# A graph attention network on one core: the order of the weight loads, the place of two weighed tiles, and a third transpose buffer

## The chip, the cores and the metric

The kernel runs on one core of a Trainium2 chip. The metric is the device time of one launch in microseconds. All durations below come from one profiled execution of the kernel before the change, unless a median of runs is named.

## What is computed

Two graph attention layers over 512 nodes with 768 features, then a residual and a layer norm. The first layer has eight heads, the second has one. Cut to what matters:

```python
def gat_layer(x, W, a_s, a_d, b, edge_index, concat):
    h = (x @ W).reshape(n, H, C)                       # 512 x 768 per head
    alpha_s = einsum('nhc,hc->nh', h, a_s)
    alpha_d = einsum('nhc,hc->nh', h, a_d)
    e = leaky_relu(alpha_s[src] + alpha_d[dst], 0.2)
    e = exp(e - segment_max(e, dst)[dst])
    alpha = e / (segment_sum(e, dst)[dst] + 1e-16)
    out = segment_sum(h[src] * alpha[:, :, None], dst)
    return out + b                                     # heads side by side

h   = elu(gat_layer(x, W1, a_src1, a_dst1, b1))        # W1: 768 x 6144
out = gat_layer(h, W2, a_src2, a_dst2, b2)             # W2: 6144 x 768
return layernorm(x + out)
```

## The kernel before

The edges are counted once into a dense 512 x 512 matrix `cnt` (from destination to source). With it the attention of one head is a dense softmax: `lift` adds the two logits into a tile `q[t]` of 128 destinations x 512 sources, `leak` and `rank` apply the leaky ReLU and the maximum on DVE and the exponential on ACT, and `weigh` multiplies by `cnt`, sums, and divides. There are four such tiles per head, t = 0 to 3. Each must then be transposed into `PT`. `turn_out` does the first half of that: ACT copies the tile into `nr` with its 16-bit halves apart (L548), and the SP queue issues a DMA transpose from `nr` into `zr` (L550). `turn_in` does the second half: ACT copies `zr` into `PT` (L553). Both `nr` and `zr` have two buffers, and the same names are used as scratch by `elu` and `mixed`.

The dense products are done by a scheme with seven half-size products in place of eight. A product is a sequence of fourteen "pairs": the seven products in the order P1, P2, P6, P7, P4, P5, P3, each for row blocks i = 0 and 1. A pair has a part on TensorE (six matmuls, L248) and an emptying part (DVE or ACT), called m and e here. P2 adds to the PSUM bank of P1, P4 to that of P7, P3 to that of P5, and each of these needs the bank's first result taken out before it starts. So P3 of block i cannot start until DVE has run L286, the emptying of P5, on the same block.

For each head there are three stages of TensorE work, and the loop over h runs them in this order for different heads:

- `mixed(h, ...)` (L625): attention times features of head h, then the ELU.
- `second(h, ...)` (L248, `gT` and `gS` operands): the result times the 768 x 768 block `W2[h]`, added into `h2`.
- `projection(h + 2, ...)` (L248, `xT` and `xS` operands): x times the block `W1[h + 2]`.

During `second(h)` the tiles `q[t]` of head h + 1 are made: the loop over n = 2 to 6 runs pairs 2n and 2n + 1, so that n = 5 holds P5 and n = 6 holds P3. Tiles 0 and 1 are weighed and turned out in n = 4 and 5. Tile 2 follows in n = 6, between the two emptyings of P3. Tile 3 follows in step n = 0 of the loop over `projection`. After it, in the same step, `load_w2(h + 1)` is issued.

A weight block is held in three tiles. `W[h][0]` and `W[h][1]` are its upper and lower 384 rows, loaded by three DMAs each. `t1` is a 384 x 384 block: first a copy of the upper left block by the SP queue (L109), then the upper right block added by an accumulating DMA on the POOL queue (L110), which must wait until the copy has landed. `rest` then adds the lower right block into the right half of `W[h][0]` with a second accumulating DMA (L115). The tiles of W1 are in the slots named `w2`, those of W2 in the slots named `w1`, and each slot has one buffer. So in the profile `w1t` is `t1` (and the sums t2 and t4) of a W2 block, and `w2t` the same of a W1 block. Two sums on DVE complete a block: L240 makes t2 from t1 and the lower right block, and L241 makes t4. For `W2[h + 1]` these two are put into the projection loop at steps n = 9 and 10, ahead of the emptyings of P5:

```python
                if n in (9, 10):
                    sums2.pop(0)()
```

The order of instructions on each engine is the order written in the program; nothing reorders them. The SP queue issues its DMAs in that order too, so a DMA that must wait for a buffer holds up those behind it.

Before the loop there is a head-0 phase. The first half of `projection(1)` is mixed with the counting; pairs 4 to 13 then run while head 0's four tiles are weighed and transposed, following the table `beside`. `load_w2(0)` is issued ahead of that phase. After pair 13 come `rsums` (L597 to L600), which make the sums of `PT` that `mixed(0)` needs.

In the last turn of the loop (h = 6) there is no projection. `load_w2(7, "w2")` loads into the W1 slots, and `a_src2` and `a_dst2` are loaded behind it. DVE then computes the logit vectors `V` from `W2[7]` (L702).

Of the kernel before, what the change touches and what calls it, by code (L numbers as in the profile page):

```python
# [8 lines left out]
F32 = mybir.dt.float32  # L9
# [3 lines left out]
U16 = mybir.dt.uint16  # L13
AF = mybir.ActivationFunctionType
ALU = mybir.AluOpType
# [21 lines left out]
def gat_pass(  # L37
# [16 lines left out]
    nc = tc.nc  # L54
    P = 128
    N, D = x.shape
# [4 lines left out]
    HALF = D // 2  # L61
    EC = E // P
    EH = EC // 2
    HK = DC // 2
    HN = N // 2
    L, R = slice(0, HALF), slice(HALF, D)
# [29 lines left out]
    W1, W2, A = {}, {}, {}  # L96

    def load_w(W, h, slot, m):


        W[h] = []
        for r in range(2):
            w = wpool.tile([P, HK, D], F32, name=f"{slot}{r}")
            for k in range(r * HK, (r + 1) * HK):
                nc.sync.dma_start(w[:, k - r * HK, :], m[k * P:(k + 1) * P, :])  # L105
            W[h].append(w)
        t1 = wpool.tile([P, HK, HALF], F32, name=f"{slot}t1")
        upper = m[:HK * P, :].rearrange("(k p) d -> p k d", p=P)
        nc.sync.dma_start(t1, upper[:, :, L])  # L109
        nc.gpsimd.dma_start(t1, upper[:, :, R], accum_op=ALU.add)  # L110
        W[h].append(t1)

        def rest():

            nc.gpsimd.dma_start(W[h][0][:, :, R], m[HK * P:, R].rearrange("(k p) d -> p k d", p=P),  # L115
                                accum_op=ALU.add)
        return rest
# [4 lines left out]
    def load_w2(h, slot="w1"):  # L122
        return load_w(W2, h, slot, w2[h * D:(h + 1) * D, :])
# [248 lines left out]
    def leak(q):  # L372
        nc.vector.scalar_tensor_tensor(q, q, NEG_SLOPE, q, op0=ALU.mult, op1=ALU.min)

    def rank(q, t):

        nmax = small.tile([P, 1], F32, name="nmax")
        nc.vector.tensor_tensor_reduce(out=q, in0=q, in1=absent[:, t, :], scale=1.0, scalar=-NO_EDGE,  # L378
                                       op0=ALU.add, op1=ALU.min, accum_out=nmax)
        nc.scalar.activation(q, q, AF.Exp, bias=nmax, scale=-1.0)  # L380
        return q
# [164 lines left out]
    def turn_out(q, t):  # L546
        apart = work.tile([P, N], F32, name="nr").bitcast(U16)
        nc.scalar.copy(apart.rearrange("p (h n) -> p h n", h=2), q.bitcast(U16).rearrange("p (n h) -> p h n", h=2))  # L548
        parted[t] = work.tile([P, N], F32, name="zr").bitcast(U16)
        nc.sync.dma_start(parted[t].rearrange("p (j d) -> p j d", d=P), apart, transpose=True)  # L550

    def turn_in(t):
        nc.scalar.copy(PT.rearrange("p s n -> p (s n)").bitcast(U16).rearrange("p (s n h) -> p s n h", s=NT, h=2)[  # L553
            :, :, t * P:(t + 1) * P, :], parted.pop(t).rearrange("p (h s d) -> p s d h", h=2, s=NT))

    def elu(h, c, z, cols, name, spare=None):

        j = h * DC + c
        n = z.shape[-1]
        neg = work.tile([P, n], F32, name=f"n{name}")  # L560
        pos = work.tile([P, n], F32, name=f"z{name}") if spare is None else spare
        nc.scalar.activation(neg, z, AF.Relu, bias=nb1T[:, j:j + 1], scale=-1.0)
        nc.scalar.activation(pos, z, AF.Relu, bias=b1T[:, j:j + 1])
        nc.scalar.activation(neg, neg, AF.Exp, scale=-1.0)
        return lambda: nc.vector.scalar_tensor_tensor(gT[:, c, cols], neg, -1.0, pos, op0=ALU.add, op1=ALU.add)
# [37 lines left out]
    def mixed(h, A_, B_, fill):  # L603

        tt = nc.vector.tensor_tensor
        behind = []

        def some(n):
            for f in fill[:n]:
                f()  # L610
            del fill[:n]

        for c in range(HK):
            u = work.tile([P, HN], F32, name="u")
            w = work.tile([P, HN], F32, name="w")
            zr = work.tile([P, N], F32, name="zr")
            bank = {}

            def part(p, over=None):
                if over is None:  # L620
                    bank[p] = mm.tile([P, 512], F32, name="mm")
                else:
                    bank[p] = bank[over]
                for k in range(2):
                    nc.tensor.matmul(bank[p][:, :HN], A_[p][:, k, c * P:(c + 1) * P], B_[p][:, k, :],  # L625
                                     start=over is None and k == 0, stop=k == 1, skip_group_check=True)
                return bank[p][:, :HN]

            nc.scalar.copy(u, part("P1"))  # L629
            if behind:  # L630

                behind = behind[0]()
            tt(u, u, part("P6"), op=ALU.add)
            tt(w, u, part("P7"), op=ALU.add)
            for f in behind[:1]:
                f()
            near_l = elu(h, c, part("P2", over="P1"), near, "l")
            some(1)
            tt(zr[:, far_], part("P5"), w, op=ALU.subtract)
            for f in behind[1:]:  # L640
                f()
            tt(zr[:, near], u, part("P4", over="P7"), op=ALU.add)
            near_l()
            tt(u, part("P3", over="P5"), u, op=ALU.subtract)
            some(-(-len(fill) // (2 * (HK - c) - 1)))

            def others(c=c, u=u, zr=zr):
                return [elu(h, HK + c, zr, slice(0, N), "r", spare=zr), elu(h, c, u, far_, "l", spare=u)]
            behind = [others]
        return behind[0]()  # L650

    load_a(1, a_src1[1], a_dst1[1])
    load_w2(0)()

    AA, lsums = left_sums(0)
    BB, rsums = right_sums()
# [2 lines left out]
    def give(t):  # L659
        weigh(q[t], t)  # L660
        turn_out(q[t], t)

    beside = {4: [lambda: give(0)], 7: [lambda: give(1)], 8: [lambda: leak(q[3]), lambda: rank(q[3], 3)],
              9: [lambda: turn_in(0), lambda: give(2)], 10: [lambda: turn_in(1), lambda: give(3)], 11: lsums[:1],
              12: [lambda: turn_in(2), *lsums[1:3]], 13: [lambda: turn_in(3), some_logits[0]]}
    for n in range(4, 14):
        pairs[n][0]()
        if n > 4:
            pairs[n - 1][1]()
        for f in beside.get(n, []):  # L670
            f()
    pairs[13][1]()
    for f in rsums:
        f()
    besides = [lsums[3], some_logits[1]]
    B2, pending = right(W2[0], "w1")
    for h in range(H - 1):
        if h + 2 < H:
            load_w1(h + 2)()
# [49 lines left out]
        for n in range(2, 7):  # L729
            (m0, e0), (m1, e1) = pairs[2 * n:2 * n + 2]  # L730
            m0()
            if not last:
                m1()
            if n < 6:
                leak(q[n - 2])
                rank(q[n - 2], n - 2)
            if n < 5:
                q.append(lift(h + 1, n - 1))
            if last:

                if n > 3:
                    turn(q[n - 4], n - 4)
                if n == 6:
                    weigh(q[3], 3)
                m1(lambda: turn(q[3], 3) if n == 6 else None)
            e0()
            if last and 2 < n < 6:
                weigh(q[n - 3], n - 3)
            if not last and n > 3:
                weigh(q[n - 4], n - 4)  # L750
                if n == 6:
                    turn_in(0)
                turn_out(q[n - 4], n - 4)
            e1()
        if h + 2 < H:
            B_, sums = right(W1[h + 2], "w2")
            pairs = projection(h + 2, XA, B_)
            for n in range(14):
                pairs[n][0]()
                if n == 0:  # L760
                    weigh(q[3], 3)
                    turn_in(1)
                    turn_out(q[3], 3)
                    load_w2(h + 1)()
                    B2, sums2 = right(W2[h + 1], "w1")
                if n in (1, 3):
                    sums[n // 2]()
                if n == 1:
                    AA, sums3 = left_sums(h + 1) if h + 3 < H else (None, [])
                pairs[n][1]()  # L770
                if n in (2, 4):
                    turn_in(1 + n // 2)
                if n == 5 and h + 3 < H:
                    BB, sums3 = right_sums()
                if 1 <= n < 9 and h + 3 < H:
                    sums3.pop(0)()
                if n in (9, 10):
                    sums2.pop(0)()
                if n in (11, 13):
                    logits(h + 2, HS[h + 2], 2 + (n - 11) // 2)  # L780
        else:
            last_sum()
            B2, sums2 = right(W2[H - 1], "w1")
# [151 lines left out]
```

## Time and profile before

| | us |
|---|---|
| median of 3 runs | 701.91 (701.33 to 703.17) |
| profiled execution | 701.47 |
| its span | 699.6 |
| TensorE busy | 663.7 |
| DVE busy | 511.7 |
| ACT busy | 248.3 |
| POOL busy | 41.8 |
| mean granted TensorE clock | 0.979 |

The span is the time from the first to the last recorded instruction; 1.87 us of the profiled execution lie around it. In the profile's rows, "L248" is a line of the kernel before, PE is TensorE's matmuls, PEld its weight loads, and a letter q after an engine means the engine's queue of DMA issues and waits. A DMA row in the chain of waits lasts from the issue to the landing. `mm` is a PSUM bank, `hs` the features of a head, `pS` the sums of `PT`.

### The profile page before, as it was taken

The page shows a single profiled execution, that of the slowest core. Times are in us where ns is not written, and L with a number is a line of the kernel's source. Part 1 is how long each engine was busy: PE and PEld are TensorE (multiplying, and loading weights), DVE is VectorE, ACT ScalarE, POOL GpSimd, SP SyncE. Part 2 cuts the span into 40 slices and gives each one's busy share as a digit, 9 for nine tenths or more (in the row PEclk, how much of TensorE's full clock was granted, in tenths as well). Part 3 has the DMA queues.
Part 4 walks back from the last instruction along what each step waited for, and adds up shares of the span by engine and source line. Part 5 has one row for each costly group of instructions (what it writes and reads, how often), then busy time and mean ns, then how long its engine had stood idle before and what let it go on. Part 6 is the DMA issues. An engine that isn't in the chain of part 4 may idle for free.

```text
span 699.6 us, 7102 instructions
## 1 busy us (share of the span) xinstructions
PE 663.7 (95%) x2419; PEld 406.5 (58%) x2419; DVE 511.7 (73%) x1102; ACT 248.3 (35%) x417; POOL 41.8 (6%) x52
## 2 busy tenths in 40 slices
PE   9999969997999989997999989997999989999995
PEld 4554557554865557554865567554865544554653
DVE  6899959965778577865778477775778179868685
ACT  2212536340545116340545116340545114234340
POOL 1200110001100101001100101001100101000000
PEclk9999989999999999999999999999999999999999
DMA  8705765076612855066612855076713866100021
GB/s 312 202 4 175 138 201 111 16 205 145 167 48 52 268 145 115 15 202 148 171 44 55 266 145 113 15 209 141 176 39 60 264 173 154 42 0 1 15 68 72
DMA packets 71355, 85.58 MB, mean 122 GB/s; under 512 B 36566, under 2 KB 55950, under 8 KB 71310
## 3 DMA queue, kind: packets, MB, share of 16 engines
q1 hardware_dynamic: 59022, 66.76, 30.9%
q0 software_dynamic: 12000, 17.70, 15.6%
q10 hardware_dynamic: 288, 0.59, 0.2%
q8 instruction: 21, 0.34, 0.2%
q14 instruction: 24, 0.20, 0.1%
HBM read 75.07 MB, written 1.57 MB: 110 GB/s over the span
## 4 chain that ended last, share of the span: by engine, by line
PE 76%; DMA 15%; DVE 4%; SPq 2%; issue 2%; ACT 1%; POOLq 0%; DVEq 0%; ACTq 0%
PE mm L248 42%; PE mm L625 16%; DMA w1t<-in_L_gnn_W_dram 13%; PE mm L571 5%; PE mm L352 5%; PE mm L887 3%; SPq L105 2%; PE tr L430 2%; DMA zr<-nr 2%; DVE w1t L240 1%; PE bc L154 1%; PE bc L430 1%; PE bc L363 0%; DVE scr L702 0%; DVE hs L286 0%
## 5 line engine op out<-in xcount | busy, mean ns | idle before, releaser
L248 PE MATMUL mm<-w,gT 128*128 128x384 f32 x288 | 97.7, 487 | 0.3 <-DVE u L306 0.3
L248 PE MATMUL mm<-w,xT 128*128 128x384 f32 x252 | 84.8, 489 | 0.0
L248 PEld LDWEIGHTS mm<-w,gT 128*128 128x128 f32 x288 | 53.4, 190 | 36.9 <-DVE u L306 2.6
L248 PEld LDWEIGHTS mm<-w,xT 128*128 128x128 f32 x252 | 47.2, 190 | 35.1 <-ACT hs L281 3.0
L248 PE MATMUL mm<-w1t,gS 128*128 128x384 f32 x180 | 60.7, 486 | 0.0
L248 PE MATMUL mm<-w,xS 128*128 128x384 f32 x84 | 39.0, 631 | 21.0 <-DVE hs L286 21.0
L629 ACT COPY u<-mm 128x256 f32<-128x256 f32 x18 | 6.7, 372 | 145.2 <-PE mm L625 145.2
L380 ACT ACTIVATE q<-q,nmax 128x512 f32<-128x512 f32 x36 | 25.8, 722 | 90.3 <-DVE nmax L378 90.3
L248 PE MATMUL mm<-w2t,xS 128*128 128x384 f32 x168 | 56.6, 487 | 0.0
L306 DVE TENSOR_TENSOR h<-h,mm 128x384 f32<-128x384 f32 x72 | 39.7, 551 | 20.5 <-PE mm L248 19.3
L625 PE MATMUL mm<-PT,hs 128*128 128x256 f32 x216 | 54.0, 387 | 0.0
L248 PEld LDWEIGHTS mm<-w1t,gS 128*128 128x128 f32 x180 | 34.1, 190 | 23.6
L625 PEld LDWEIGHTS mm<-PT,hs 128*128 128x128 f32 x216 | 42.1, 195 | 7.5 <-issue 0.4
L248 PEld LDWEIGHTS mm<-w2t,xS 128*128 128x128 f32 x168 | 31.8, 190 | 22.2 <-issue 0.2
L625 PE MATMUL mm<-pS,gS 128*128 128x256 f32 x144 | 38.0, 387 | 5.5 <-DVE pS L598 5.5
L248 PEld LDWEIGHTS mm<-w,xS 128*128 128x128 f32 x84 | 20.1, 245 | 39.8 <-DVE hs L286 24.7
L548 ACT COPY nr<-q 128x1024 uint16<-128x1024 uint16 x32 | 33.4, 1043 | 25.6 <-DVE q L534 25.6
L571 PE MATMUL mm<-PT,hs 128*128 128x512 f32 x96 | 41.6, 593 | 0.0
L553 ACT COPY PT<-zr 128x1024 uint16<-128x1024 uint16 x32 | 37.1, 1158 | 8.1 <-DMA zr<-nr 8.1
L418 DVE TENSOR_SCALAR os<-nodes,idx 128x512 bf16<-128x512 f16 x132 | 35.5, 340 | 3.6 <-PE tr L430 3.6
L625 PEld LDWEIGHTS mm<-pS,gS 128*128 128x128 f32 x144 | 27.8, 194 | 9.7 <-DVE pS L598 5.9
L352 PE MATMUL mm<-w,xT 128*128 128x384 f32 x96 | 33.2, 493 | 0.0
(158 smaller groups left out, 1048.1 us busy)
## 6 DMA issues: line engine op xcount, KB each, us to landing
w<-in_L_gnn_W_dram SPq DMA_DIRECT2D x90, 384.0 KB, 5.6
w<-in_L_gnn_W_dram POOLq DMA_DIRECT2D x15, 576.0 KB, 10.2
w2t<-in_L_gnn_W_dram SPq DMA_DIRECT2D x8, 576.0 KB, 6.1
w2t<-in_L_gnn_W_dram POOLq DMA_DIRECT2D x8, 576.0 KB, 6.3
w1t<-in_L_gnn_W_dram SPq DMA_DIRECT2D x7, 576.0 KB, 8.8
w1t<-in_L_gnn_W_dram POOLq DMA_DIRECT2D x7, 576.0 KB, 7.9
a_s<-in_L_gnn_a_src_dram SPq DMA_DIRECT2D x8, 384.0 KB, 6.8
a_d<-in_L_gnn_a_dst_dram SPq DMA_DIRECT2D x8, 384.0 KB, 6.3
```

What stands on the lines that cost most here:

```text
L105: nc.sync.dma_start(w[:, k - r * HK, :], m[k * P:(k + 1) * P, :])
L248: nc.tensor.matmul(ps[:, :HALF], A_[p][:, k, i * P:(i + 1) * P], B_[p][:, k, :], start=start and k == 0, stop=k == HK - 1, skip_group_chec ...
L306: nc.vector.tensor_tensor(a, a, ps, op=ALU.subtract if p == "P7" else ALU.add)
L352: nc.tensor.matmul(ps, xT[:, r * HK + k, t * P:(t + 1) * P], W1[h][r][:, k, cols], start=r == 0 and k == 0, stop=r == 1 and k == HK - 1)
L380: nc.scalar.activation(q, q, AF.Exp, bias=nmax, scale=-1.0)
L418: nc.vector.tensor_scalar(hot[c], nodes, idx[:, 1, c:c + 1], None, op0=ALU.is_equal)
L430: nc.tensor.matmul(cps[t][r:r + B, :N], od[:, c, k * B:(k + 1) * B], hot[c], start=todo[b] == hits[b], stop=todo[b] == 1, tile_position=(0 ...
L548: nc.scalar.copy(apart.rearrange("p (h n) -> p h n", h=2), q.bitcast(U16).rearrange("p (n h) -> p h n", h=2))
L553: nc.scalar.copy(PT.rearrange("p s n -> p (s n)").bitcast(U16).rearrange("p (s n h) -> p s n h", s=NT, h=2)[:, :, t * P:(t + 1) * P, :], p ...
L571: nc.tensor.matmul(ps[:, :N], HS[h][:, s, c * P:(c + 1) * P], PT[:, s, :], start=(s == 0), stop=(s == NT - 1))
L625: nc.tensor.matmul(bank[p][:, :HN], A_[p][:, k, c * P:(c + 1) * P], B_[p][:, k, :], start=over is None and k == 0, stop=k == 1, skip_group ...
L887: nc.tensor.matmul(ps[:, :cols.stop - cols.start], PT[:, s, t * P:(t + 1) * P], h2[:, s, cols], start=(s == 2), stop=(s == 1))
```

## The change

Four things are moved; every computation and every transfer stays.

1. In `load_w` the copy and the accumulation of `t1` come first, ahead of the six DMAs of `W[h][0]` and `W[h][1]`. This holds for W1 and W2 blocks alike.
2. In the loop, tile 2 is weighed and turned out ahead of the emptying of P3's block 0, and tile 3 between the two emptyings of P3, both in n = 6. `load_w2(h + 1)` follows there. The step n = 0 of the projection keeps only `turn_in(1)`.
3. In the head-0 phase `load_w2(0)` moves behind the issue of head 0's fourth transpose (n = 10). The tiles 2 and 3 are given one step earlier relative to the emptyings, and the `turn_in`s are placed anew.
4. `zr` gets a third buffer (in `turn_out`, and in the two other places that use the name, `elu` and `mixed`).

```diff
     def load_w(W, h, slot, m):
+        t1 = wpool.tile([P, HK, HALF], F32, name=f"{slot}t1")
+        upper = m[:HK * P, :].rearrange("(k p) d -> p k d", p=P)
+        nc.sync.dma_start(t1, upper[:, :, L])
+        nc.gpsimd.dma_start(t1, upper[:, :, R], accum_op=ALU.add)
         W[h] = []
         for r in range(2):
             w = wpool.tile([P, HK, D], F32, name=f"{slot}{r}")
             for k in range(r * HK, (r + 1) * HK):
                 nc.sync.dma_start(w[:, k - r * HK, :], m[k * P:(k + 1) * P, :])
             W[h].append(w)
-        t1 = wpool.tile([P, HK, HALF], F32, name=f"{slot}t1")
-        upper = m[:HK * P, :].rearrange("(k p) d -> p k d", p=P)
-        nc.sync.dma_start(t1, upper[:, :, L])
-        nc.gpsimd.dma_start(t1, upper[:, :, R], accum_op=ALU.add)
         W[h].append(t1)
...
-        parted[t] = work.tile([P, N], F32, name="zr").bitcast(U16)
+        parted[t] = work.tile([P, N], F32, name="zr", bufs=3).bitcast(U16)
...
     load_a(1, a_src1[1], a_dst1[1])
-    load_w2(0)()
...
-    beside = {4: [lambda: give(0)], 7: [lambda: give(1)], 8: [lambda: leak(q[3]), lambda: rank(q[3], 3)],
-              9: [lambda: turn_in(0), lambda: give(2)], 10: [lambda: turn_in(1), lambda: give(3)], 11: lsums[:1],
-              12: [lambda: turn_in(2), *lsums[1:3]], 13: [lambda: turn_in(3), some_logits[0]]}
+    done = {n: (lambda n=n: pairs[n][1]()) for n in range(4, 13)}
+    beside = {4: [lambda: give(0)], 5: [done[4]], 6: [done[5]], 7: [done[6], lambda: give(1)],
+              8: [done[7], lambda: leak(q[3]), lambda: rank(q[3], 3), lambda: turn_in(0)], 9: [lambda: give(2), done[8]],
+              10: [lambda: give(3), lambda: turn_in(1), done[9]], 11: [done[10], lsums[0]],
+              12: [done[11], lambda: turn_in(2), *lsums[1:3]], 13: [done[12], some_logits[0], lambda: turn_in(3)]}
     for n in range(4, 14):
         pairs[n][0]()
-        if n > 4:
-            pairs[n - 1][1]()
-        for f in beside.get(n, []):
+        for f in beside[n]:
             f()
+        if n == 10:
+            load_w2(0)()
+            B2, pending = right(W2[0], "w1")
...
+            if not last and n == 6:
+                turn_in(0)
+                weigh(q[2], 2)
+                turn_out(q[2], 2)
             e0()
             if last and 2 < n < 6:
                 weigh(q[n - 3], n - 3)
-            if not last and n > 3:
+            if not last and 3 < n < 6:
                 weigh(q[n - 4], n - 4)
-                if n == 6:
-                    turn_in(0)
                 turn_out(q[n - 4], n - 4)
+            if not last and n == 6:
+                weigh(q[3], 3)
+                turn_out(q[3], 3)
+                load_w2(h + 1)()
             e1()
...
                 if n == 0:
-                    weigh(q[3], 3)
                     turn_in(1)
-                    turn_out(q[3], 3)
-                    load_w2(h + 1)()
                     B2, sums2 = right(W2[h + 1], "w1")
```

More of the change, by code (lines that the diff above doesn't have):

```diff
@@ L560, in elu @@
         neg = work.tile([P, n], F32, name=f"n{name}")
-        pos = work.tile([P, n], F32, name=f"z{name}") if spare is None else spare
+        pos = work.tile([P, n], F32, name=f"z{name}", bufs=3 if name == "r" else 2) if spare is None else spare
         nc.scalar.activation(neg, z, AF.Relu, bias=nb1T[:, j:j + 1], scale=-1.0)
@@ L615, in mixed @@
             w = work.tile([P, HN], F32, name="w")
-            zr = work.tile([P, N], F32, name="zr")
+            zr = work.tile([P, N], F32, name="zr", bufs=3)
             bank = {}
@@ L675, in gat_pass @@
     besides = [lsums[3], some_logits[1]]
-    B2, pending = right(W2[0], "w1")
     for h in range(H - 1):
```

## The prediction

> **What bounds the kernel now.** I read the page first, then the waits of PE, then the chain of waits, then the timelines of SP, DVE and PE around one stall.
>
> ```profile
> PE 663.7 (95%) x2419; PEld 406.5 (58%) x2419; DVE 511.7 (73%) x1102; ACT 248.3 (35%) x417; POOL 41.8 (6%) x52
> ...
> PE mm L248 <- DVE hs L286: 21.0, 6, 4.0
> PE mm L625 <- DVE pS L598: 5.5, 1, 5.5
> ```
>
> TensorE is busy 95% of the span, and its idle time is nearly all in two places: six waits for L286 (once per turn of the loop with a projection) and one for `pS` in the head-0 phase. Only what shortens these can be worth much. The chain of waits in turn h = 1:
>
> ```profile
> 226.88 0.52 SPq L105
> ...
> 229.89 8.96 DMA w1t<-in_L_gnn_W_dram
> 238.92 0.48 issue
> 239.41 7.52 DMA w1t<-in_L_gnn_W_dram
> 246.96 1.36 DVE w1t L240
> 248.32 0.48 DVE hs L286
> 248.84 5.83 PE mm L248 x12
> 254.67 18.38 PE mm L625 x84
> ```
>
> SP issues six W DMAs, then the copy of `t1`; it lands after 8.96, POOL adds to it for 7.52, then DVE can run L240. L240 stands in DVE's order ahead of L286, which P3 needs. So P3 waits for a transfer that it does not use. Its own block then takes 5.83 instead of the 4.03 of the other blocks of twelve:
>
> ```profile
> 241.54 4.03 PE L248 MATMUL mm<-w2t,xS 128*128 128x384 f32 x12
> 248.84 5.83 PE L248 MATMUL mm<-w,xS 128*128 128x384 f32 x12 [3.27 <-DVE hs L286]
> ...
> 248.00:252.00 4.00, 3.16 (x7) 1.88 (x8) 3.96 (x7) 0.00 (x0) 0.00 (x0) 0.76 0.19 32
> ```
>
> The last row is a stretch of the windows view: the granted clock falls to 0.76 behind the stall. The head-0 phase in the chain:
>
> ```profile
> 75.81 9.39 DMA zr<-nr
> ...
> 89.37 3.05 DMA zr<-nr
> 92.45 1.17 ACT PT L553
> 93.64 0.70 DVE pS L597
> 94.36 0.70 DVE pS L598
> 95.11 20.38 PE mm L625 x80
> ```
>
> The first transpose lands after 9.39, the others' best is 3.05: it was issued while `load_w2(0)`'s two accumulations ran.
>
> **Part 1 and 2: the loop.** Worth at most: blocks of twelve start 3.87 apart when nothing waits (237.67, 241.54), so from the start of P5 to the start of `mixed` 7.74 are needed. The PE timeline shows 13.67, 12.97, 13.39, 12.74, 13.43 and 13.05 in the six turns; lost 5.93 + 5.23 + 5.65 + 5.00 + 5.69 + 5.31 = 32.8. That is idle time plus cold matmuls.
>
> How much earlier `t1` comes, in turn h = 1:
> - DVE. One `weigh` takes 1.51 (220.78 to 222.29). Tile 2's now starts where L306 of P5 ends, 218.97, and ends 220.5; P3's first emptying 221.0; tile 3's `weigh` 222.5 (before 224.3); the second emptying 223.0 (before 222.8). Projection's P1 needs neither of these two banks, so nothing waits for the 0.2.
> - ACT. `turn_in(0)` ends 220.65, tile 2's copy 221.7. Tile 3's copy needs the `nr` of tile 1, whose transpose goes out at 219.6 and takes 3.05: it runs 222.7 to 223.7. `turn_in(1)` now stands behind it and ends 224.9, then L281 ends 225.3; P2 needs that at 225.84. No wait.
> - SP. The last transpose goes out at 223.7 and occupies SP for 1.23. The third `zr` buffer is what lets tile 2's go out without waiting for `turn_in(0)`. `t1` is issued at 224.95 instead of 229.89. Its buffer is free: P5 of `second(1)` ended at 218.3. `W[h][1]`, used by P3 until 222.1, is free too. So SP is not blocked.
> - Copy of `t1`: between 4.0 (the single x tile on ACT's queue, smaller) and 8.96 (behind six others). It now has only a transpose in front; I take 5.0: landed 230.0, POOL's issue 0.5, accumulation from 230.5.
> - Accumulation: the row is 7.52, beside three W DMAs (longest 8.85, the shortest for `w2t` 5.7). Now up to six W DMAs share the queues. The Trainium skill, DMA: Bandwidth & Descriptors, section on queues, rings and completion order, says that each DMA engine takes turns between queues packet by packet, which speaks against this change: SP's burst, which stood before the accumulation, is now beside it. By the rule: 80 to 84 us moved 165 GB/s with the engines full of accumulations, so 0.59 MB is 3.6 of engine time; shared half and half 7.2, with about 2.7 for start and receipt (6.3 typical for `w2t`, less 3.6) 9.9: landed 240.4. By the row: 238.0. I take the rule's.
> - The six W DMAs (L240 reads `W[h][1]`): the same 2.95 MB start 1.9 earlier; the last landed by 238.85, now 236.9 plus 3.6 for the accumulation in between: 240.5.
>
> L240's place in DVE's order comes at 242.3, behind L285. P3 would start at 245.41, so L240 must start by 245.41 - 1.36 - 0.48 - 0.04 = 243.5. Data at 240.5 leave 3.0 of margin. Even 8.96 and 8.85 together give 224.95 + 8.96 + 0.48 + 8.85 = 243.3. So all of the stall goes: -32.8. L241 then lies between the two L286, which P3's second block needs only at 247.3. The next limit is PE's own stream.
>
> Also moved: `load_w1(h + 2)` now begins with `t1`, freed by P5 (245.4), so its six DMAs go out then instead of from 237.86 and 256. They are needed some 50 us later; behind them on SP are only `a_s` and `a_d`, and on POOL its two accumulations. Cost 0. The same reorder at the start (`load_w1(1)`) is needed at 63.2 and was in at 27.3 + 10.2 (POOL's last addition, median to landing) = 37.5: 0.
>
> **Part 3: head 0.** `mixed(0)` took 26.79 (88.54 to 115.33) against 18.38 later: 8.4 lost. Without accumulations beside it the first transpose lands in 3.05 (bounds: 1.23 or again 4.05 of issue, its own row). Copies follow at ACT's pace, the fourth transpose out at 84.0 to 85.4, `turn_in(3)` ends 88.3 to 89.7. DVE reaches `rsums` at 89.2, after L287 of pair 13, so L598 ends 90.4 to 91.0, while PE finishes P1 of `mixed` at 89.4: idle 1.1 to 1.7. The skill, TensorE: Matmul & The Clock Gate, Part 1, puts the cold clock behind an idle window of about 3.4; the trace shows it already behind 3.04 (turn h = 3). At 1.1 neither makes it cold; if it did, the 2.4 of before (5.04 for twelve matmuls worth 2.6) would stay. I take -7.0 (ends -4.5 and -7.3).
>
> `load_w2(0)` moves from 60.6 to about 85, with `load_w1(2)` right behind: 5.9 MB at 366 GB/s (window 232 to 236) is 16.1, four accumulations at 3.6 14.4; all is in by 118. `W2[0]` comes first in both queues, by about 103; P1 needs it at 110, L240 at 116. Cost 0; uncovered, each us late costs one.
>
> **The last turn.** `load_w2(7)` now starts with `t1`, which waits for P5 of the last projection. Before, `W[7][0]` was issued at P7's end (552.01), 17 us ahead of `W[7][1]`.
>
> ```profile
> 570.72 0.48 SPq L685 DMA_DIRECT2D w2t<-in_L_gnn_a_src_dram  x1
> ...
> 578.67 0.96 DVE L702 SCALAR_TENSOR_TENSOR scr<-w,w2t 128x768 bf16<-128x768 f32 x1 [0.37 <-DMA w2t<-in_L_gnn_a_dst_dram]
> ...
> 596.05 2.20 PE L248 MATMUL mm<-w,gT 128*128 128x384 f32 x6 [0.32 <-DVE u L306]
> ```
>
> DVE waits for `a_src2` and is then full until PE waits for it, so a later `a_src2` is paid in full. With E the end of P3: before, 568.7 + 9.9. Now `t1`, `W[7][0]`, `W[7][1]` and `a_src2` (3.3 MB, 9.1 at 366 GB/s) and 3.6 to 3.9 of accumulation run from E - 1.8: E + 11.2, with the receipt E + 12.2. Cost +2.3 (ends 0, if DMA has slack there, and +4).
>
> **Sum.** Against the profiled execution: 701.47 - 32.8 - 7.0 + 2.3 = 664.0. The median is 0.44 above it: 664.4. I predict 664.4.
>
> **The rivals.**
> - *Part of the wait stays.* The accumulation or `W[h][1]` lands 1 to 3 after the deadline, so L240 is still last. For: six W DMAs beside it have no row. Against: the 3.0 of margin. A stall of 2 per turn leaves 12, to 676; with the cold block 23, to 687. Chance 0.17.
> - *The accumulation is starved: slower.* Place: L240 in each of six turns. Decides: what head 0 and the last turn net is 7.0 - 2.3 = 4.7, 0.8 per turn; so if the data come over 0.8 later than before, past 247.8, all is lost. From 230.5 that is an accumulation of 17.3, twice the longest row. At 19 it is 1.7 x 6 = 10 minus 4.7: 707. For: POOL's is one ring against a queue of six loads. Against: in 240 to 244 it got its share beside three. Chance 0.05.
> - *The reorder moves nothing in the loop:* `W[h][1]` was the late one all along and lands when it did, with only head 0 gained: 701.9 - 4.7 = 697. Against: the waits name `w1t`, landed 8 us later. Chance 0.04.
>
> **Chances.** The forecast 0.74. About 0.3% (2 us) can be told from no change in this kernel. Faster 0.93, same 0.02 (starved just so), slower 0.05. The forecast's own ends: 701.9 - 32.8 - 7.3 = 661.8, and -32.8 - 4.5 + 4 = 668.6. PE's weight loads also waited 3.0 in all for L281, which comes 0.5 earlier in each turn: up to -3 more. The range takes in that end and the first half of the first rival: 659 to 679.
>
> **What would show it.** Right: no wait of PE for L286 over 0.5, block P3 at 4.03, `t1` issued by SP before the six W DMAs and 5 us earlier against P5, turns of 73.0 instead of 78.4, `mixed(0)` under 20, and L702 waiting about 2.5. Wrong: L240 waiting for `w1t` or `w` past the end of P5; PE waiting for W2's first block in `second(0)`; a granted clock under 0.95 in the middle of the loop.

## The result and the profile after

| | us |
|---|---|
| before, median of 4 runs beside it | 701.62 (701.21 to 703.17) |
| after, median of 4 runs | 661.37 (660.9 to 662.61) |
| ratio after / before | 0.9425, 95% interval 0.9405 to 0.9445 |
| profiled execution of after | 662.61 |
| its span | 660.8 (699.6 before) |
| mean granted TensorE clock | 0.996 (0.979 before) |

The page of after, first the engines, then the shares of the chain of work that ended last:

```profile
PE 649.1 (98%) x2419; PEld 401.1 (61%) x2419; DVE 511.7 (77%) x1102; ACT 248.6 (38%) x417; POOL 42.8 (6%) x52
...
PE 93%; DMA 3%; DVE 2%; issue 1%; SPq 0%; ACT 0%; DVEq 0%
```

TensorE runs the same 2419 matmuls in 14.6 us less busy time, nearly all of it because the blocks behind the old stalls are no longer cold: six times 1.8, and 2.3 in `mixed(0)`. The waits of PE in after (in total, times, longest):

```profile
PE mm L248 <- DVE u L306: 1.4, 2, 0.8
...
PE mm L625 <- DVE pS L598: 1.1, 1, 1.1
```

The row for L286 (21.0 us before) is gone, and the one for `pS` fell from 5.5 to 1.1. One turn of the loop in the chain of waits of after:

```profile
186.56 50.31 PE mm L248 x156
236.87 18.38 PE mm L625 x84
255.25 3.87 PE mm L248 x12
```

156 matmuls of `second` and `projection` follow one another without a gap, where before a transfer, a POOL addition, L240 and L286 stood in the middle. The same turn in the timelines, SP first, then PE, then DVE:

```profile
203.32 9.32 SPq L550 DMA_TRANSPOSE zr<-nr  x4
212.74 0.52 SPq L103 DMA_DIRECT2D w1t<-in_L_gnn_W_dram  x1
213.35 3.20 SPq L109 DMA_DIRECT2D w<-in_L_gnn_W_dram  x6
...
228.97 4.03 PE L248 MATMUL mm<-w2t,xS 128*128 128x384 f32 x12
232.84 4.03 PE L248 MATMUL mm<-w,xS 128*128 128x384 f32 x12
...
229.64 1.35 DVE L240 TENSOR_TENSOR w1t<-w1t,w 128x1152 f32<-128x1152 f32 x1
231.10 0.56 DVE L286 TENSOR_TENSOR hs<-mm,hs 128x384 f32<-128x384 f32 x1
```

`t1` is issued in front of the six loads, 16.23 ahead of P5's start (212.74 to 228.97; before 229.89 to 241.54, which is 11.65). A square bracket behind a row would name what the engine waited for; L240 carries none, so its data is there. Block P3 is at 4.03, and the first matmul of `mixed` starts at 236.71 in the PE timeline: 7.74 behind P5's start, the distance when nothing waits. (The chain, in which ends are followed, has 236.87 for it.)

How the 38.8 of span divide, each from the same two points of the PE timelines: the loop -32.8 (the six distances P5 to `mixed` are all 7.74); `mixed(0)` -6.8 (26.79 to 20.02); the first two blocks of `projection` -0.9 in all (8.05 to 7.90 in each of six turns, the weight loads' wait for L281); the last turn +1.3 (start of `mixed` to P6 of `second(7)`: 29.36 to 30.70); the start of the program +0.4.

### The profile page after: what moved, and what is told of

Read it like the earlier page. It is cut to its first block, busy times and chain, and to the rows that moved or that the text cites. A ratio compares the mean times of both kernels' runs of the same rounds, so it can differ in the third digit from the quotient of the medians.

```text
span 660.8 us, 7107 instructions
## 1 busy us (share of the span) xinstructions
PE 649.1 (98%) x2419; PEld 401.1 (61%) x2419; DVE 511.7 (77%) x1102; ACT 248.6 (38%) x417; POOL 42.8 (6%) x52
## 4 chain that ended last, share of the span: by engine, by line
PE 93%; DMA 3%; DVE 2%; issue 1%; SPq 0%; ACT 0%; DVEq 0%
PE mm L248 61%; PE mm L625 17%; PE mm L352 5%; PE mm L571 3%; PE mm L891 3%; PE tr L430 2%; DMA w2t<-in_L_gnn_a_dst_dram 2%; DMA hs<-in_x_dram 1%; DVE scr L703 1%; PE bc L430 1%; PE bc L363 0%; DVE gT L565 0%; PE mm L327 0%; PE tr L819 0%; PE tr L540 0%
## 5 line engine op out<-in xcount | busy, mean ns | idle before, releaser
L248 PE MATMUL mm<-w,gT 128*128 128x384 f32 x288 | 97.8, 488 | 1.4 <-DVE u L306 1.4
L248 PE MATMUL mm<-w,xT 128*128 128x384 f32 x252 | 83.9, 487 | 0.0
L248 PEld LDWEIGHTS mm<-w,gT 128*128 128x128 f32 x288 | 53.4, 190 | 38.2 <-DVE u L306 3.9
L248 PEld LDWEIGHTS mm<-w,xT 128*128 128x128 f32 x252 | 47.7, 190 | 33.7 <-issue 0.4
L248 PE MATMUL mm<-w1t,gS 128*128 128x384 f32 x180 | 60.7, 486 | 0.0
L248 PE MATMUL mm<-w2t,xS 128*128 128x384 f32 x168 | 56.6, 487 | 0.0
L625 PE MATMUL mm<-PT,hs 128*128 128x256 f32 x216 | 52.5, 379 | 0.0
L306 DVE TENSOR_TENSOR h<-h,mm 128x384 f32<-128x384 f32 x72 | 39.7, 551 | 13.9 <-PE mm L248 12.7
L248 PEld LDWEIGHTS mm<-w1t,gS 128*128 128x128 f32 x180 | 34.1, 190 | 23.6
L248 PEld LDWEIGHTS mm<-w2t,xS 128*128 128x128 f32 x168 | 31.8, 190 | 22.2 <-issue 0.2
L625 PEld LDWEIGHTS mm<-PT,hs 128*128 128x128 f32 x216 | 41.0, 190 | 6.9
L553 ACT COPY PT<-zr 128x1024 uint16<-128x1024 uint16 x32 | 37.1, 1159 | 2.0 <-DMA zr<-nr 2.0
L248 PE MATMUL mm<-w,gS 128*128 128x384 f32 x96 | 32.6, 486 | 0.0
L248 PE MATMUL mm<-w1t,gT 128*128 128x384 f32 x96 | 32.5, 487 | 0.0
L571 PEld LDWEIGHTS mm<-PT,hs 128*128 128x128 f32 x96 | 18.2, 190 | 22.9 <-issue 21.5
```

Source lines behind the costliest of these rows:

```text
L248: nc.tensor.matmul(ps[:, :HALF], A_[p][:, k, i * P:(i + 1) * P], B_[p][:, k, :], start=start and k == 0, stop=k == HK - 1, skip_group_chec ...
L306: nc.vector.tensor_tensor(a, a, ps, op=ALU.subtract if p == "P7" else ALU.add)
L571: nc.tensor.matmul(ps[:, :N], HS[h][:, s, c * P:(c + 1) * P], PT[:, s, :], start=(s == 0), stop=(s == NT - 1))
```

## The experiments

All are timed against the kernel before, run beside them on the same chip. In the first group one part of the change is made alone, in the kernel before.

**Part 1 alone: `t1` first in `load_w`.**

```diff
     def load_w(W, h, slot, m):
+        t1 = wpool.tile(...)
+        nc.sync.dma_start(t1, upper[:, :, L])
+        nc.gpsimd.dma_start(t1, upper[:, :, R], accum_op=ALU.add)
         W[h] = []
...
-        t1 = wpool.tile(...)
-        nc.sync.dma_start(t1, upper[:, :, L])
-        nc.gpsimd.dma_start(t1, upper[:, :, R], accum_op=ALU.add)
         W[h].append(t1)
```

> The kernel before with part 1 alone: t1 is copied and added first in every weight load; tiles, head-0 phase and zr buffers as before. Theory (L240 waits for t1, and the order of the load is enough): in turn h = 1 t1 is issued at 226.9 where the six W DMAs began, lands in 4.5, the accumulation takes about 9, so the data are there at 240.5 to 241.5, ahead of the 243.5 at which L240 must start. All 32.8 of the loop go, the last turn costs 1.3, head 0 keeps its loss or part of it: 664 to 670. Rival (the tiles' earlier place is what brings t1 forward): at most a third of the 32.8 goes: over 690.

Measured: 662.59 (662.25 to 662.81), ratio 0.9434 (0.9386 to 0.9483): as far as the intervals can tell, the whole change (0.9425). In turn h = 1, from its SP, POOL and DVE timelines:

```profile
214.41 0.52 SPq L103 DMA_DIRECT2D w1t<-in_L_gnn_W_dram  x1
...
219.35 1.28 POOL L104 DMA_DIRECT2D w1t<-in_L_gnn_W_dram  x1 [49.67 <-DMA w1t<-in_L_gnn_W_dram]
...
229.73 1.35 DVE L240 TENSOR_TENSOR w1t<-w1t,w 128x1152 f32<-128x1152 f32 x1
```

The reorder gains twice. `t1` is issued 14.65 ahead of P5's start (229.06) instead of 11.65, and its copy no longer lands behind six loads: 4.94 from issue to POOL's start, against 9.5 before (229.89 to 239.41). Together the accumulation can begin 7.6 sooner. Part 1 reorders the W1 blocks too: the next block's loads now go out at 233.60, where before three of them were issued 1.55 ahead of the accumulation, and part 2 below shows that such loads delay it. How much of the gain comes from that, no run separates.

It also mends head 0, which I had put down to part 3. `t1` of `W2[0]` is now first there as well, so the two accumulations start at 67.26 and 70.53 instead of at 73.44 and 74.23; POOL's queue has moved 0.83 MB of their 1.18 MB by 76, when the first transpose goes out (76.03), and the rest by 78. In the kernel before they run from 75 to 83. The DMA view of before for 76 to 82 (q0 is POOL's queue, q1 SP's; the columns are packets, MB and the time of the packets as a share of the 16 engines) shows what the first transpose, issued at 75.81, had to wait for:

```profile
q0 software_dynamic: 670, 1.00, 102.2%
q1 hardware_dynamic: 234, 0.06, 7.8%
```

The four transposes of `zr` in this phase, by the tile view of the kernel before:

```profile
DMA to landing us min/median/max: 3.0/5.3/9.4
```

and by that of part 1 alone:

```profile
DMA to landing us min/median/max: 3.1/3.4/3.6
```

The 9.4 is gone, L598 starts at 90.15 (before 94.36), and PE's wait for `pS` is 1.1, the same as in after.

**Part 2 alone, with the third buffer: tiles 2 and 3 weighed around P3, `t1` last.**

```diff
+            if not last and n == 6:
+                turn_in(0)
+                weigh(q[2], 2)
+                turn_out(q[2], 2)
             e0()
...
+            if not last and n == 6:
+                weigh(q[3], 3)
+                turn_out(q[3], 3)
+                load_w2(h + 1)()
             e1()
```

> The kernel before with part 2 alone: tiles 2 and 3 weighed around P3, load_w2(h + 1) behind them, third zr buffer; t1 is loaded last and the head-0 phase is as before. Theory: t1 is issued about 2 earlier than before, its data are there at about 245 to 246, 1.4 to 2.7 past the deadline, so L286 stays late but by less; 678 to 687 if a wait that short leaves TensorE's clock up, 690 to 697 if P3's block still takes 5.83. Rival (either part alone is enough): 669 or less.

Measured: 699.19 (694.67 to 702.69), ratio 0.9954 (0.9926 to 0.9982). Neither expectation holds. The profiled execution is the slowest of the ten (702.69), and in it the wait for L286 is not smaller at all:

```profile
PE mm L248 <- DVE hs L286: 21.6, 6, 4.1
```

Turn h = 1 in its chain of waits:

```profile
228.81 9.16 DMA w1t<-in_L_gnn_W_dram
...
238.53 9.69 DMA w1t<-in_L_gnn_W_dram
248.24 1.36 DVE w1t L240
```

P5 starts at 241.94 here, so `t1` is issued 13.13 ahead of it: 1.5 earlier than before, as planned. But the accumulation takes 9.69 where it took 7.52, and over all seven blocks the medians to landing are 8.7 and 9.4, against 8.8 and 7.9. What was won at the issue was given back in the accumulation. What differs beside it is the next block's first three loads (`load_w1`, issued when PE frees their buffer): before they were issued 1.55 ahead of the accumulation (237.86 and 239.41), here 0.27 ahead (238.26 and 238.53). The DMA view of this kernel for 238 to 243 shows the cause:

```profile
q1 hardware_dynamic: 340, 0.95, 67.1%
q0 software_dynamic: 1, 0.00, 0.2%
```

While these loads ran on SP's queue, the accumulation issued at 238.53 moved one packet; it ran from 243 on, when they were nearly over. In before the loads were over about a microsecond earlier, and POOL's queue began then, at 242 to 243. Where the 2.5 of the medians lies, this execution does not show, apart from 0.9 (the first two blocks of `projection` take 7.90 here too).

**Part 3 alone, with the third buffer: `load_w2(0)` behind the transposes and the new table `beside`.**

```diff
     load_a(1, a_src1[1], a_dst1[1])
-    load_w2(0)()
...
+        if n == 10:
+            load_w2(0)()
```

> The kernel before with part 3 alone: the head-0 phase and the place of load_w2(0) as in the changed kernel, with the third zr buffer; the loop and the order inside a load as before. Theory: the first transpose lands in about 3 instead of 9.4, mixed(0) takes 20.0 instead of 26.8, the loop's waits stay: 694.8. Rival (W2(0), now 25 later and with t1 last, is late for second(0)): 697 or more, with a wait of PE for L306 or for w in second(0).

Measured: 695.94 (694.08 to 697.56), ratio 0.9917 (0.9885 to 0.995). The `pS` wait is 1.1, the waits for L286 stay (22.5 in all). Standing alone, part 3 brings 5.8 of the 7.0 worked out for it; beside part 1 there is nothing left for it to win, since each gives the same 1.1.

**The sums later, nothing else.** L240 and L241 are moved behind both emptyings of P5 in DVE's order; no transfer moves.

```diff
-                if n in (9, 10):
+                if n in (12, 13):
                     sums2.pop(0)()
```

> The kernel before with one edit: the two sums of W2[h + 1] stand at steps 12 and 13 of the projection loop instead of 9 and 10; no transfer is moved. Theory (P3 waited only because L240 stood ahead of L286 in DVE's order): PE's wait for L286 is gone and P3's block takes 4.03; DVE then has 2.7 of sums to do where mixed begins, so a new wait in mixed of at most 2.7 in each turn: 680 to 688, or less if mixed has slack. Rival (the transfer itself bounds the turn): 699 to 702.

Measured: 674.2 (673.0 to 674.54), ratio 0.9598 (0.9547 to 0.9648). PE's waits in this kernel:

```profile
PE mm L625 <- DVE pS L598: 5.0, 1, 5.0
PE mm L625 <- DVE w L634: 2.7, 5, 0.5
```

Turn h = 1 in its PE timeline:

```profile
236.53 4.03 PE L248 MATMUL mm<-w2t,xS 128*128 128x384 f32 x12
240.40 4.03 PE L248 MATMUL mm<-w,xS 128*128 128x384 f32 x12
244.27 1.03 PE L625 MATMUL mm<-PT,hs 128*128 128x256 f32 x4
```

The waits for L286 are gone and P5 to `mixed` is 7.74, although `t1` is as late as ever. So the stall was not TensorE waiting for data: it was L286 standing behind an instruction that waited for data. The price is that the two sums now stand in front of L633 and L634, which `mixed` needs: PE waits for L634 in five turns, and `mixed` takes 19.54 (244.27 to 263.81) instead of 18.38. Head 0's wait stays, as nothing was done about it.

The second group undoes or adds one thing in the kernel after. On the chip of the first three of them after itself gave 661.46 (660.89 to 662.34) in a second run, ratio 0.9426 (0.9399 to 0.9452).

> The changed kernel once more, as the yardstick of the three runs beside it: 661.4.

Its last turn is 29.48 from `mixed` to P6 of `second(7)`, against 30.70 in the first profile of the same kernel and 29.36 before. So this stretch differs by 1.2 from one execution to another.

**`t1` last in `load_w2(7)` alone.**

```diff
     def load_w2(h, slot="w1"):
-        return load_w(W2, h, slot, w2[h * D:(h + 1) * D, :])
+        return load_w(W2, h, slot, w2[h * D:(h + 1) * D, :], late=h == H - 1)
```

(`late` puts the two DMAs of `t1` behind the six loads.)

> The changed kernel, but load_w2(7) in the last turn copies and adds t1 last, as before the change. Theory (t1 first holds up a_src2 in the last turn, and PE pays for it): L703 waits 0.4 instead of 2.1 and 1.0 to 1.4 is gained: 660.2. Rival (that delay is covered): no change, 661.4.

Measured: 661.49 (661.36 to 661.8), ratio 0.9424 (0.9398 to 0.9449); the last turn is 29.37. No difference in time that can be told.

**`a_src2` and `a_dst2` ahead of `load_w2(7)`.**

```diff
-            last_sum = load_w2(H - 1, "w2")
             A[H] = []
             for j, a in ((2, a_src2[0]), (4, a_dst2[0])):
...
+            last_sum = load_w2(H - 1, "w2")
```

> The changed kernel, with a_src2 and a_dst2 issued ahead of load_w2(7) instead of behind it. Theory: they land before L703 needs them, DVE does not wait there, and PE's two waits for L306 in the last turn (0.54 and 0.85) go: 1.4 to 2.0 gained, 659.6. Rival (W2[7]'s own rows come as late): no more than with the old order of t1, 660.2 or above.

Measured: 661.41 (661.26 to 661.97), ratio 0.9425 (0.9399 to 0.9451); the last turn is 29.36. No difference that can be told.

**The same, and L597 and L598 ahead of pair 13's emptying in head 0.**

```diff
+    for f in rsums[:2]:
+        f()
     pairs[13][1]()
-    for f in rsums:
+    for f in rsums[2:]:
         f()
```

> As the run before this one, and the first two sums of PT (L597, L598) stand ahead of the emptying of pair 13 in the head-0 phase. Theory: PE's wait of 1.1 for L598 shrinks to about 0.2, and everything else stays: 658.7. Rival (the bank that pair 13 holds longer is then missed by mixed): 659.6 or more.

Measured: 660.83 (660.65 to 661.18), ratio 0.9414 (0.9388 to 0.944). The `pS` wait fell from 1.1 to 0.3. It is the lowest median of all, 0.6 below after, about what one wait of 0.8 is worth. The ratios' intervals overlap, but they carry the scatter of the kernel before: all five runs lie below all five of the kernel without this last move (661.26 to 661.97).

**Two `zr` buffers instead of three**, in all three places that use the name; the cut shows one.

```diff
-        parted[t] = work.tile([P, N], F32, name="zr", bufs=3).bitcast(U16)
+        parted[t] = work.tile([P, N], F32, name="zr").bitcast(U16)
```

> The changed kernel with two zr buffers again. ACT's order has turn_in(0) ahead of tile 2's copy, but turn_in(1) behind tile 3's copy, so tile 3's transpose must wait for turn_in(1): about 1.1 later in each turn, and all loads with it. Theory: the margin in front of L240 covers it, head 0 loses 0.2 to 1.1: 661.4 to 662.5. Rival (the third buffer is needed): 665 or more.

Measured: 661.62 (660.96 to 662.8), ratio 0.9413 (0.9384 to 0.9443). The third buffer is not needed. In turn h = 1 `t1` is issued 15.12 ahead of P5's start instead of 16.23, because tile 3's transpose now waits for `turn_in(1)`; the margin in front of L240 covers that.

**More traffic beside the accumulation.** Eight loads of 384 KB are put on SP's queue behind the six of each `W2` block from h = 1. They read rows of that block and write them to the output tensor, which the last stage overwrites; nothing of the computation waits for them. With three lines added, L240, L248, L286 and L550 are L243, L251, L289 and L553 here.

```diff
+        if slot == "w1" and h:
+            for k in range(8):
+                nc.sync.dma_start(out[k % NT * P:(k % NT + 1) * P, :], m[k % NT * P:(k % NT + 1) * P, :])
         W[h].append(t1)
```

> The changed kernel with eight more DMAs of 384 KB on the SP queue behind the six of each W2 block from h = 1 on (rows of W2 to the output tensor, which the end of the kernel overwrites). They do not stand ahead of anything L240 needs; they only keep SP's queue full while POOL accumulates. Theory (the two queues take turns, so the accumulation keeps its share): t1 is complete 0 to 4 later, the margin of 3.4 covers all or nearly all: 661 to 666. Rival (an accumulation is starved while SP's queue has work): t1 is complete 8 or more later, PE waits 4 to 5 for L286 in each turn and its clock falls: 690 or more.

Measured: 689.63 (684.67 to 693.96), ratio 0.9801 (0.9743 to 0.9859). In turn h = 1 `t1` is again issued first, at 217.46. The chain of waits of this kernel:

```profile
222.34 16.65 DMA w1t<-in_L_gnn_W_dram
...
239.01 1.36 DVE w1t L243
240.37 0.48 DVE hs L289
```

Block P3 in its PE timeline, of the same turn and of a later one:

```profile
240.89 5.83 PE L251 MATMUL mm<-w,xS 128*128 128x384 f32 x12 [3.16 <-DVE hs L289]
...
553.72 4.14 PE L251 MATMUL mm<-w,xS 128*128 128x384 f32 x12 [2.02 <-DVE hs L289]
```

With 3.1 MB more on the other queue the accumulation takes 16.65 instead of the 9.4 that is after's median, and the old stall is back, by the old road: L243 waits, L289 stands behind it, PE waits for L289. The rival of starvation, which I had at 0.05, is real; the change escapes it only because its six loads are over in time. The windows view of after shows that. Its columns are the stretch, its length, busy time (and instructions) of PE, PEld, DVE, ACT and POOL, the granted clock, the DMA share and GB/s:

```profile
216.00:218.00 2.00, 2.00 (x7) 1.14 (x6) 0.00 (x0) 1.60 (x4) 0.04 (x1) 1.00 1.04 411
...
222.00:224.00 2.00, 2.00 (x8) 1.21 (x7) 1.29 (x4) 0.00 (x0) 0.18 (x1) 1.00 1.08 193
224.00:226.00 2.00, 2.00 (x7) 1.14 (x6) 1.22 (x3) 0.00 (x0) 0.00 (x0) 1.00 1.16 202
```

Plain loads move 411 GB/s, accumulations about 200. Which queue moved the bytes is in the DMA view, for 218 to 222, where only SP's queue has a row, and for 222 to 228:

```profile
q1 hardware_dynamic: 578, 1.58, 102.2%
...
q0 software_dynamic: 710, 1.07, 107.2%
q1 hardware_dynamic: 53, 0.11, 5.2%
```

POOL issued the accumulation at 217.96, but its queue moved nothing until the loads were over, some 4 us later; then it had the engines nearly to itself, for this accumulation and that of `rest` (L115, issued at 220.90). The wait is more than an empty start: in before, with no loads beside it, an accumulation issued at 262.29 moved its first bytes between 264 and 265. With the extra traffic, for 222 to 226, again with a row of SP's queue alone, and for 226 to 238:

```profile
q1 hardware_dynamic: 599, 1.63, 103.5%
...
q1 hardware_dynamic: 366, 3.47, 72.7%
q0 software_dynamic: 494, 0.74, 35.2%
```

Here POOL's queue begins some 5 us behind its issue, and then SP's queue is not empty: of the 4.2 MB moved up to 238, POOL's two accumulations got 0.74.

## Why the prediction was right, and where it was wrong

**The loop, -32.8: right, to the tenth.** The six distances from P5 to `mixed` are 7.74, no wait for L286 is left, the turns are 73.0, and block P3 is at 4.03, as the last part of the prediction asked. That the stall came from L240's place in front of L286, and not from P3's own data, is shown by the sums put later: the same stall goes while every transfer stays.

**`t1` 4.9 earlier: 4.6 measured** (16.23 against 11.65 ahead of P5). Part 1 gives 3.0 of it and part 2 1.5, by the two kernels with one part each. The prediction treated the two as one step. The runs separate them: part 1 alone brings the whole gain, part 2 alone 2.5 of the 40, with the waits for L286 as long as before.

**The copy in 5.0: right.** The median to landing is 4.5, where it was 8.8 behind the loads:

```profile
w1t<-in_L_gnn_W_dram SPq DMA_DIRECT2D x7, 576.0 KB, 4.5
w1t<-in_L_gnn_W_dram POOLq DMA_DIRECT2D x7, 576.0 KB, 9.4
```

**The accumulation in 9.9: right in size (9.4), by luck; its working was wrong.** I took the rule of the Trainium skill, DMA: Bandwidth & Descriptors, section on queues, rings and completion order, that an engine takes turns between queues, and made of it a half share. In after there was no sharing to see: nothing for some 4 us, then all. With eight more loads a half share of 7.2 plus 2.7 would still be 9.9; the run shows 16.65, and 18% of the bytes. Turns need not be halves of the bytes: in that stretch the profile counts 366 packets with 3.47 MB for SP's queue and 494 with 0.74 MB for POOL's. What held the accumulation back altogether at first, the runs do not show.

Two readings under the estimate were off as well. From "240 to 244" I concluded that the accumulation of before "got its share beside three" loads, but from 239 to 242 POOL's queue moved nothing, and the loads were over when it began. And the stretch 80 to 84 held transposes beside the accumulations: alone they move 0.41 MB in 2 us (226 to 228 in after), so 0.59 MB is 2.9 of engine time and not 3.6.

The margin, 3.0 in the prediction, is 4.4 in turn h = 1: landed at 217.96 + 8.6 = 226.56, where L240 would have to start by 232.84 - 1.36 - 0.48 - 0.04 = 230.96. Over the six turns it is 3.8 to 4.8.

**Head 0, -7.0: right in size (-6.8), and in the wait that is left (1.1); the owner was wrong.** In turn 0 of the chain of waits of after DVE reaches the sums behind L287, as worked out:

```profile
89.16 0.56 DVE hs L287
89.72 0.61 DVE pS L597
90.35 0.70 DVE pS L598
91.10 18.04 PE mm L625 x80
```

But part 1, which also moves `W2[0]`'s accumulations 6.2 and 3.7 forward, brings this gain without part 3. I had followed the reorder into `load_w1(1)` at the start and not into `load_w2(0)`. "`mixed(0)` under 20" was just missed, with 20.02.

The prediction weighed the clock gate here (the Trainium skill, TensorE: Matmul & The Clock Gate, Part 1: cold behind an idle window of about 3.4). The runs give no such limit. The first turn of the traffic run and the last turn of part 3 alone, in their PE timelines:

```profile
162.77 5.83 PE L251 MATMUL mm<-w,xS 128*128 128x384 f32 x12 [2.66 <-DVE hs L289]
...
559.45 4.14 PE L248 MATMUL mm<-w,xS 128*128 128x384 f32 x12 [3.21 <-DVE hs L286]
```

The first block is cold behind 2.66 (granted clock 0.65 from 162 to 166), the second is not, behind 3.21 (1.00 from 559 to 563). After the wait of 1.1 in head 0 the next four matmuls took 1.13, against 1.03 when nothing waits, in every run that has it.

**The last turn, +2.3: the mis-sized term.** Measured +1.3 in the first profile, +0.1 in the second of the same kernel, and 0.0 in the two that undo it. DVE's waits for `a_src2` and `a_dst2` in after, on DVE's timeline:

```profile
539.89 0.96 DVE L703 SCALAR_TENSOR_TENSOR scr<-w,w2t 128x768 bf16<-128x768 f32 x1 [1.61 <-DMA w2t<-in_L_gnn_a_src_dram]
...
541.37 0.96 DVE L703 SCALAR_TENSOR_TENSOR scr<-w,w2t 128x768 bf16<-128x768 f32 x1 [0.52 <-DMA w2t<-in_L_gnn_a_dst_dram]
```

The wait of about 2.5 that I foresaw is 2.1 in this execution. In the second profile only 1.00 is left, for `a_dst2`, and PE waits 0.43. "DVE is then full until PE waits for it, so a later `a_src2` is paid in full" was the step that failed: of 2.1 late at most 1.3 reached PE. That there is a cost at all is shown by PE's waits for L306: 0.4 to 1.6 in the five profiles with `t1` first and `a_src2` last in this turn, 0.3 where either is undone and in before.

**The third buffer: wrong.** "The third `zr` buffer is what lets tile 2's go out without waiting for `turn_in(0)`": with two buffers the time is the same. In ACT's written order `turn_in(0)` stands ahead of tile 2's copy anyway, so its buffer is free by then. It is tile 3's transpose that the third buffer lets out, 1.1 earlier, and nothing waited for that.

**L281, "up to -3 more": -0.9.** The wait of the weight loads went in each turn, but only 0.15 of its half microsecond was on TensorE's path.

**Together:** the sum had -37.5; the last turn came out 1.0 lower, L281 brought 0.9, head 0 was 0.2 short and the start 0.4 later, which makes the -38.8 of the spans. The predicted median, 664.4, is 3.0 above the measured one. Of that 1.4 is this sum; the rest is the step from one profiled execution to medians, which lay 0.44 above it before and 1.24 below it after (the profiled execution had the last turn's +1.3). The rivals "part of the wait stays" and "the reorder moves nothing" have no trace in after. Starvation exists, but with 3.8 us of margin or more it does not decide.

## What to carry to other kernels

When TensorE waits for a vector instruction, look at what stands ahead of that instruction on its own engine: here a sum that needed a transfer held up the emptying of a PSUM bank, and either an earlier transfer or a later sum removed the stall. Where one transfer of a batch has a second stage behind it (a copy, then an accumulation on another queue), issue it first; here that one reorder was worth 39 us, and issuing the whole batch 1.5 us sooner was worth 2.5 (by the interval, 1.3 to 5.2), with the old stall still there. Before crediting a gain to several moves made together, run each alone: as far as these runs can tell, the first of the four parts brings all of it, two bring nothing more beside it, and the third buffer nothing.

## What was not expected of the hardware

An accumulating DMA on POOL's queue moved nothing while the loads that stood ahead of it on SP's queue ran (4 us in after, 3 in before, both in turn h = 1), and then got 18% of the bytes beside further traffic (copies to the output tensor): 16.65 for 576 KB where it took 8.6 without. The other way round, the first transpose of head 0 took 9.4 while accumulations had the engines, and 3.1 to 3.6 without them. Accumulations moved about 200 GB/s with the engines full, plain loads 411; short packets alone are not the reason, for 220 to 222 of the traffic run moved 408 GB/s with 293 of its 424 packets under 2 KB. What decides between the two queues these runs do not show.
